# Letting a planned decoder kernel choose its engine for standardisation and for the addends of maxima

## The chip, the core and the metric

The kernel runs on one core of a Trainium2 chip. The metric is the device time of one execution in microseconds (us); lower is better. The core has five engines that run at the same time and meet through semaphores: TensorE (PE, with its weight loads PEld), VectorE (DVE), ScalarE (ACT), GpSimd (POOL) and SyncE (SP), whose queue issues this kernel's DMA transfers. Matrix products land in PSUM[...].

## The reference, cut to what matters

Two sequences of 512 tokens with 1024 features pass through three blocks, each with a layer normalisation ahead and a residual around it:

```python
x = x + attn(layernorm(x), ...)    # 32 heads over 8 kv heads; weights are signs times a scale; full softmax
x = x + xattn(layernorm(x), ...)   # see below
x = x + ffn(layernorm(x), ...)     # dense 1024x1024 plus low-rank products
```

```python
def rat_read(res, W, gamma, beta, num_outputs):
    x = res.reshape(b, l, H, C)                     # 256 x 4
    y = jnp.einsum('blhc,hoc->bloh', x, W)          # 3 or 2 outputs of 256
    mu = y.mean(-1, keepdims=True)
    var = y.var(-1, keepdims=True)
    yn = (y - mu) * jax.lax.rsqrt(var + EPS)        # standardisation
    return yn * gamma + beta
# xattn: rat_read (3) -> rotated causal attention, 16 heads -> rat_write (gated state update)
#        -> rat_read (2) -> silu(gate) * up -> rat_write
```

Softmax needs the maximum of each row of scores. Both attentions of each sequence are therefore made in two passes: one that finds the maxima, one that makes exponentials of the shifted scores.

## The kernel before

The work is cut into jobs, each a Python generator. A job yields `(engine, time, ready)` ahead of a group of instructions, and the planner `run` picks the job whose step can start soonest, with a `lag` added to each job's time. That fixes one order of instructions per engine, written out before anything runs: a late operand holds up what stands behind it on the same engine. The lags of jobs are in the list in `build`, those of their spawned parts in `LAGS`. `self.free[engine]` is the planned time at which an engine comes free, and some steps look at it to choose between two engines, as `emptied` does. `take` and `give` hand out rooms of a fixed number of buffers: two single PSUM banks, three PSUM pairs, four `probs`, eight pages, eleven rows, twelve slabs.

The stages, named as the tiles are (A and B, and C and D, are the two sequences):

- `in`, `k`, `v`, `q`, `wo`, `proj`: the input tiles are standardised and split into three bf16 parts, the weights turned to signs, and q, k and v projected.
- `maxA`, `maxB`: the first attention's maxima, 8 groups of 4 heads. `peaks` makes the scores of 128 queries in two PSUM pairs, and `reduced` takes the maxima of each pair on VectorE (two reductions per step).
- `turned`, once per group, splits the maxima `mx` into three bf16 addends in `parts`. TensorE transposes `parts`, and ScalarE copies them out as `shift`. In `attend`, a matmul with a constant row of ones (`ones16`) adds the shift into the scores ahead of the exponential. So the maxima can be subtracted by TensorE.
- `attA`, `attB` (`attend_1`), `outA`, `outB`: exponentials on ScalarE, products with v, sums of exponentials. For the sums, VectorE adds the four tiles of exponentials of a group into `held`, and four matmuls with `ones` sum over keys. Where VectorE is planned to be more than `SPARE` us late at the end of a group, the last tile is not added but gets its own four matmuls (`direct`).
- `factor`: low-rank products for the last block, kept in DRAM.
- `stateA`, `stateB` (`state_inputs`): each tile of 128 tokens is read back, measured (`measured`: statistics on VectorE, the inverse deviation by a logarithm and an exponential on ScalarE), standardised over 1024 features and passed to `read`, which transposes, multiplies, and standardises three times over 256. The mean and deviation are kept in `norm` for the tails.
- `maxC`, `maxD`, `attC`, `attD`: the causal attention in the same two passes, 4 groups each.
- `tailA`, `tailB` (`tails`): the state update, a second `read` with two outputs, the gated product, a second update, per tile of 128 tokens, at most three tiles at a time. `tailW` loads their weights.
- `weights`, `factorsB`, `denseA`, `denseB`: the last block.

Standardisation before, in `state_inputs` and in `read`:

```python
t = yield "DVE", 1.3, t
nc.vector.tensor_scalar(x, x, mv[:, 0, 0:1], r, ALU.subtract, ALU.mult)
...
t = yield "DVE", 0.42 * nout, t
for o in range(nout):
    nc.vector.tensor_scalar(rows[o], rows[o], mv[:, o, 0:1], rstd[:, o : o + 1], ALU.subtract, ALU.mult)
```

Nearly all instructions of VectorE, ScalarE and GpSimd carry line 51 in the profile (the helper that records them), and most matmuls line 130, so groups are told apart by their tiles.

Of the kernel before, what the change touches and what calls it, by code (L numbers as in the profile page):

```python
# [22 lines left out]
D = 1024  # L23
# [46 lines left out]
class Kernel:  # L70
# [79 lines left out]
    def constants(self):  # L150
        nc = self.nc
        self.ident = self.const([P, P], "ident")
        make_identity(nc, self.ident)
        self.ident16 = self.const([P, P], "ident16", BF16)
        nc.vector.tensor_copy(self.ident16, self.ident)
        self.ones = self.const([P, P], "ones")
        nc.gpsimd.memset(self.ones, 1.0)
        self.ones16 = self.const([P, P], "ones16", BF16)
        nc.gpsimd.memset(self.ones16, 1.0)

        self.late = []
        for i, sign in enumerate((1, -1)):
            m = self.const([P, P], f"late{i}", BF16)
            nc.gpsimd.memset(m, 0.0)
            nc.gpsimd.affine_select(
                out=m, in_=m, compare_op=ALU.is_ge, fill=-1e30,
                base=0, pattern=[[-sign, P]], channel_multiplier=sign,
            )
            self.late.append(m)
        self.parts = [self.const([P, NT, 4, 32], f"parts{i}", BF16) for i in range(2)]  # L170
        for t in self.parts:
            nc.gpsimd.memset(t, 0.0)
        self.flip = 0
# [248 lines left out]
    def output_weights(self):  # L422
# [7 lines left out]
        "added": 0.0, "ahead": 0.0, "attA.ahead": -0.1, "attA.exponentials": -0.1, "attA.finished": 0.3,  # L430
        "attB.added": 0.0, "attB.ahead": -0.3, "co.emptied": -0.1, "cv.emptied": -0.1, "denseA.summed": -0.6,
        "denseB.emptied": 0.3, "denseB.summed": -2.0, "emptied": -0.6, "exponentials": 0.3,
        "factor.put": -1.0, "finished": 0.0, "gained": -1.0, "gated": -1.0, "joined": -0.6, "k.scale_of": 0.0,
        "maxA.reduced": 0.0, "maxA.turned": -0.1, "maxB.reduced": 0.3, "maxB.turned": -0.3,
        "maxD.turned": -0.3, "outA.clean": 1.0, "outA.stored": 2.0, "outB.stored": -1.0,
        "proj0.featured": -1.0, "proj0.valued": -0.6, "proj1.featured": -1.0, "proj1.valued": -0.6,
        "q.scale_of": 0.0, "residual": 1.0, "rotated": 0.0, "stateA.emptied": -0.3, "stateA.rotated": -0.1,
        "stateB.gained": 0.0, "stateB.rotated": 0.0, "stored": 0.6, "summed": -0.6, "tableB.emptied": -2.0,
        "tailA.gained": -1.0, "tailA.residual": -2.0, "tailB.gated": -0.3, "tailB.residual": 0.0,
        "v.scale_of": 0.0, "wo.scale_of": 0.0,  # L440
    }
    SPARE = 3

# [144 lines left out]
    def turned(self, name, b, g, mx, reduced, earlier):  # L588
        nc = self.io
        yield from self.join(*earlier)  # L590
        t = yield from self.join(*reduced)
        t = yield "DVE", 1.2, t
        parts = self.parts[self.flip]
        self.flip = 1 - self.flip
        rest = self.small([P, NT, 4], "rest")
        nc.vector.tensor_scalar(parts[:, :, :, 0], mx, -1.0, None, ALU.mult)
        nc.vector.scalar_tensor_tensor(rest, mx, -1.0, parts[:, :, :, 0], ALU.mult, ALU.subtract)
        nc.vector.tensor_copy(parts[:, :, :, 1], rest)
        nc.vector.tensor_tensor(parts[:, :, :, 2], rest, parts[:, :, :, 1], ALU.subtract)
        room = yield from self.take("bank")  # L600
        t = yield "PE", 0.35, max(t, room)
        turns = self.bank([P, NT, P], BF16)
        for qt in range(NT):
            self.turn_block(turns[:, qt, :], parts[:, qt].rearrange("p j i -> p (j i)"), self.ident16)
        room = yield from self.take("shift")
        t = yield "ACT", 0.59, max(t, room)
        shift = self.sb.tile([P, S], BF16, tag="shift", name=self._name("shift"), bufs=8)
        nc.scalar.copy(shift, turns.rearrange("p a b -> p (a b)"))
        self.give("bank", t)
        self.shifts[b][g] = shift  # L610
        self.when[f"{name}.{g}"] = t
        return t

    def attend(self, groups, operands, scale, causal):
# [4 lines left out]
        nc = self.io  # L619
# [19 lines left out]
        def probabilities(g, kt):  # L639
            if kt == 0:  # L640
                ops[g] = yield from operands(g)
            q, k, _, shift, ready, release, _ = ops[g]
            q0 = kt * P if causal else 0
            room = yield from self.take("pair", 2)
            rp = yield from self.take("probs")
            t = yield "PE", 1.46 * width[kt] + (0.1 if causal else 0.0), max(ready, room)
            s = self.scores(
                lambda j: k(j, kt * P, (kt + 1) * P), lambda j: q(j, q0, S), slice(q0, S), False
            )
            for j in range(4):  # L650
                r = slice(32 * j, 32 * j + 3)
                self.mm(
                    s[j // 2][:, j % 2, q0:], lhsT=self.ones16[r, :], rhs=shift[r, q0:], start=False, stop=True
                )
            if kt == NT - 1:
                release(t)
                self.give("shift", t)
            p = self.probs([P, 4, S])
            return p, self.spawn(exponentials(p, s, q0, max(t, rp)))
# [44 lines left out]
        for n, (g, kt) in enumerate(steps):  # L704
# [273 lines left out]
    def measured(self, parts, t):  # L978
# [13 lines left out]
        nc.scalar.activation(r, r, AF.Exp, scale=-0.5)  # L992
        return mv, r, t

    def read(self, x, t, w, gb, nout, dst, wide):


        nc = self.io
        n = nout * 32
        kind = "row" if nout == 2 else "page"  # L1000
        if wide:
# [13 lines left out]
            t = max(t, first)  # L1015
# [36 lines left out]
            self.give("page", done)  # L1052
        rows = [yn[:, o].rearrange("p a c h -> p (a c h)") for o in range(nout)]
        mv, rstd, t = yield from self.measured([[r] for r in rows], t)
        t = yield "DVE", 0.42 * nout, t
        for o in range(nout):
            nc.vector.tensor_scalar(
                rows[o], rows[o], mv[:, o, 0:1], rstd[:, o : o + 1], ALU.subtract, ALU.mult
            )
        yn = yn.rearrange("p o a c h -> p (o a c h)")  # L1060
        per = 8 if wide else 4
        ends = []
# [42 lines left out]
    def state_inputs(self, b, wide):  # L1105
# [10 lines left out]
        def tile_of(q):  # L1116
# [2 lines left out]
            x = self.page([P, D])  # L1119
            t = yield from self.fetch(x, self.kept[b][q][:, :], 512, max(ready, room))  # L1120
            mv, r, t = yield from self.measured([[x[:, :512], x[:, 512:]]], t)
            t = yield "DVE", 1.3, t
            nc.vector.tensor_scalar(x, x, mv[:, 0, 0:1], r, ALU.subtract, ALU.mult)
            keep = self.small([P, 2], "norm", bufs=8)
            nc.vector.tensor_copy(keep[:, 1:2], r)
            nc.vector.tensor_scalar(keep[:, 0:1], mv[:, 0, 0:1], r, -1.0, ALU.mult, ALU.mult)
            self.norm[b][q] = keep
            t = yield from self.read(
                x, max(t, weights), self.wr1, self.gb1, 3, lambda c: ys[c // 2][:, c % 2, q * P : (q + 1) * P], wide
# [526 lines left out]
    def build(self):  # L1656
# [31 lines left out]
                ("attA", self.attend_1(0, "maxA"), 0.0, "maxA.0"),  # L1688
                ("maxB", self.peaks_1(1), 0.0, "attA.scores"),
                ("outA", self.output_1(0), 0.0, "attA", "wo", "co"),  # L1690
                ("attB", self.attend_1(1, "maxB"), -1.0, "maxB"),
                ("tableA", self.rotation_table(0), 0.5, "attB.1"),
                ("tableB", self.rotation_table(1), 0.0, "attB.3"),
                ("stateW", self.state_weights(), 3.0, "attB.5"),
                ("outB", self.output_1(1), 0.5, "attB"),
                ("stateA", self.state_inputs(0, True), 0.2, "attB.scores"),
                ("maxC", self.peaks_2(0, "stateA"), 0.5, "stateA"),
                ("stateB", self.state_inputs(1, False), 0.5, "outB"),
                ("factor", self.factors(), -0.5, "maxB.3"),
                ("attC", self.attend_2(0, "maxC"), 0.2, "maxC.0"),  # L1700
                ("factorsB", self.factors_back(), 0.2, "attD"),
                ("maxD", self.peaks_2(1, "stateB"), 0.5, "stateB", "attC.scores"),
                ("tailW", self.tail_weights(), -0.5, "attC", "stateB"),
                ("tailA", self.tails(0), 0.5, "attC", "tailW"),
                ("attD", self.attend_2(1, "maxD"), 0.2, "maxD.1"),
                ("weights", self.dense_weights(), 0.2, "attD", "attC"),
                ("tailB", self.tails(1), 0.0, "attD", "tailW"),
                ("denseA", self.dense_all(0, "tailA"), 0.5, "tailA.0"),
                ("denseB", self.dense_all(1, "tailB"), 0.2, "tailB.0"),
            ]  # L1710
# [105 lines left out]
```

## Time and profile before

| | |
|---|---|
| median of 3 runs | 1136.23 us (1135.48 to 1136.71) |
| the profiled execution | 1135.51 us, of which the span from first to last instruction is 1133.8 us |
| mean granted TensorE clock | 0.965 |
| PE, PEld busy | 1063.1 us (94%), 521.5 us (46%) |
| DVE, ACT, POOL busy | 841.2 us (74%), 442.8 us (39%), 239.2 us (21%) |
| DMA | 70.51 MB, mean 62 GB/s |
| stages (from the trace) | maxA to 215, attA to 300, maxB with outA and factor to 430, attB to 535, stateA and outB to about 610, maxC and stateB to 662, attC and stateB to 725, maxD to 785, tails and dense to 1134 |

A time is compared with the profiled execution's own 1135.51 us. Busy shares are averages over stages with different limits: a stage's own windows say which engine fills it. "Idle before, and what ended it" names the operation that came last before an engine could go on. The granted clock is a share of full TensorE speed: where it is 0.9, a matmul takes longer than elsewhere.

### The profile page before, as it was taken

The numbers are of one execution on the slowest core, as the hardware profiler recorded it, in microseconds if no ns is written. First come the engines' busy times: TensorE is split into PE (matmuls) and PEld (weight loads), VectorE is DVE, ScalarE is ACT, GpSimd is POOL, SyncE is SP. The second block draws the span as 40 slices with busy tenths as digits, with TensorE's granted clock in tenths as the row PEclk, the third lists the DMA queues.
The fourth block names the chain that finished last, engine by engine and source line by source line (L and its number), as shares of the span: only waits on it lengthen the run. The fifth ranks groups of instructions, "written<-read, shape, count | busy, mean of one in ns | idle before, by whom it ended". The sixth has DMA issues, their size and how long they took to land.

```text
span 1133.8 us, 16121 instructions
## 1 busy us (share of the span) xinstructions
PE 1063.1 (94%) x6364; PEld 521.5 (46%) x6364; DVE 841.2 (74%) x1390; ACT 442.8 (39%) x711; POOL 239.2 (21%) x249
## 2 busy tenths in 40 slices
PE   4889999999999998999999899989988899999998
PEld 3554353333233632332555543545465465665643
DVE  7978888578878865887777961599668677788572
ACT  6762101388500215786221255224743232332310
POOL 3442333322222303454451012001200000000000
PEclk9999999999998997999999889979998999999999
DMA  6621000101214221240113000410151001011110
GB/s 256 203 82 28 20 10 20 29 20 29 61 33 177 95 64 39 61 168 1 38 56 116 8 11 16 172 38 1 57 197 68 33 20 55 11 48 38 38 37 38
DMA packets 24784, 70.51 MB, mean 62 GB/s; under 512 B 5234, under 2 KB 5252, under 8 KB 23684
## 3 DMA queue, kind: packets, MB, share of 16 engines
q1 hardware_dynamic: 24708, 69.48, 17.9%
q8 instruction: 50, 0.82, 0.3%
q14 instruction: 26, 0.21, 0.1%
HBM read 50.59 MB, written 10.49 MB: 54 GB/s over the span
## 4 chain that ended last, share of the span: by engine, by line
PE 79%; DVE 11%; ACT 5%; issue 2%; DMA 1%; POOL 1%; SPq 0%; ACTq 0%; DVEq 0%; POOLq 0%
PE proj_bank L130 8%; PE denseA_pair L130 6%; PE denseB_pair L130 6%; PE attA_pair L130 4%; PE outA_bank L130 4%; PE attB_pair L130 4%; PE tailB_bank L130 3%; PE attB_bank L130 3%; PE attA_bank L130 3%; PE maxB_pair L130 3%; PE maxA_pair L130 3%; PE tailA_bank L130 3%; PE outB_bank L130 3%; PE stateB_bank L130 3%; PE tailB_pair L130 3%; PE tailA_pair L130 3%
## 5 line engine op out<-in xcount | busy, mean ns | idle before, releaser
L51 DVE TENSOR_REDUCE maxB_mx<-maxB_pair 128x2 f32<-128x1024 f32 x64 | 75.3, 1217 | 21.7 <-PE maxB_pair L130 21.3
L51 DVE TENSOR_REDUCE maxA_mx<-maxA_pair 128x2 f32<-128x1024 f32 x64 | 75.5, 1216 | 14.0 <-PE maxA_pair L130 14.0
L130 PEld LDWEIGHTS <-start_slab 128*128 128x128 bf16 x480 | 44.7, 98 | 68.8 <-issue 21.1
L51 DVE TENSOR_TENSOR attB_probs<-attB_probs,attB_probs 128x1024 f32<-128x1024 f32 x46 | 62.6, 1401 | 13.8 <-PE attB_bank L130 13.5
L51 ACT ACTIVATE attB_probs<-attB_pair 128x1024 f32<-128x1024 f32 x64 | 62.6, 1023 | 20.9 <-PE attB_pair L130 10.8
L51 DVE TENSOR_TENSOR attA_probs<-attA_probs,attA_probs 128x1024 f32<-128x1024 f32 x46 | 56.6, 1282 | 16.9 <-PE attA_bank L130 8.5
L51 ACT ACTIVATE attA_probs<-attA_pair 128x1024 f32<-128x1024 f32 x64 | 62.1, 1021 | 9.7 <-PE attA_pair L130 9.4
L130 PE MATMUL proj_bank<-in_slab,start_slab 128*128 128x512 bf16 x240 | 55.5, 379 | 1.7 <-ACT in_slab L51 1.7
L130 PE MATMUL proj_bank<-in_probs,start_slab 128*128 128x512 bf16 x240 | 54.7, 380 | 0.0
L130 PE MATMUL maxB_pair<-maxB_row,proj_slab 32*128 32x512 f32 x256 | 47.4, 687 | 3.1 <-DVE maxB_mx L51 3.1
L51 POOL TENSOR_SCALAR proj_row<-proj_row 128x512 f32<-128x512 f32 x24 | 47.7, 1987 | 1.9
L130 PE MATMUL outA_bank<-wo_slab,attA_slab 128*128 128x512 bf16 x192 | 46.7, 392 | 0.7 <-ACT maxB_shift L51 0.7
L130 PE MATMUL attB_pair<-proj_slab,attB_row 32*128 32x512 f32 x256 | 46.7, 685 | 0.0
L51 ACT ACTIVATE proj_row<-proj_bank,cs 128x512 f32<-128x512 f32 x20 | 13.7, 686 | 80.8 <-PE proj_bank L130 60.2
L130 PE MATMUL outB_bank<-wo_slab,attB_slab 128*128 128x512 bf16 x192 | 43.3, 379 | 0.3 <-POOL attB_slab L51 0.3
L130 PE MATMUL attA_pair<-proj_slab,attA_row 32*128 32x512 f32 x256 | 41.6, 639 | 0.3 <-ACT attA_probs L51 0.3
L51 POOL MEMSET tailB_row<- 9x128 f32 x8 | 1.6, 195 | 186.4 <-PE tailB_bank L133 70.7
L130 PE MATMUL attB_bank<-attB_probs,proj_slab 128*32 128x512 f32 x256 | 38.4, 633 | 1.1 <-DVE tableA_slab L51 0.7
L51 ACT COPY maxB_shift<-maxB_bank 128x512 bf16<-128x512 bf16 x8 | 4.7, 586 | 84.7 <-PE maxB_bank L133 84.7
L51 POOL TENSOR_SCALAR proj_slab<-proj_row 128x512 f32<-128x512 f32 x24 | 14.9, 621 | 106.6 <-ACT proj_row L51 89.0
L130 PE MATMUL maxA_pair<-maxA_row,proj_slab 32*128 32x512 f32 x256 | 36.8, 640 | 0.0
L51 POOL TENSOR_SCALAR_AFFINE_SELECT attD_probs<-attD_probs 128x512 f32<-128x512 f32 x16 | 12.1, 754 | 113.8 <-ACT attD_probs L51 104.3
(410 smaller groups left out, 2321.8 us busy)
## 6 DMA issues: line engine op xcount, KB each, us to landing
in_page<-in_x_dram SPq DMA_DIRECT2D x8, 512.0 KB, 4.1
q_page<-in_q_weight_dram SPq DMA_DIRECT2D x8, 512.0 KB, 5.3
wo_page<-in_o_weight_dram SPq DMA_DIRECT2D x8, 512.0 KB, 3.4
tailW_slab<-in_write_dram SPq DMA_DIRECT2D x3, 752.0 KB, 7.1
maxA_row<-proj_slab SPq DMA_DIRECT2D x32, 64.0 KB, 2.0
attA_row<-proj_slab SPq DMA_DIRECT2D x32, 64.0 KB, 2.0
maxB_row<-proj_slab SPq DMA_DIRECT2D x32, 64.0 KB, 2.0
outA_page<-in_x_dram SPq DMA_DIRECT2D x4, 512.0 KB, 3.7
```

The source lines that it names most:

```text
L51: return self.kernel.pin(getattr(self.engine, name)(*args, **kw))
L130: self.pin(self.nc.tensor.matmul(*args, **kw))
```

## The change

Five things are changed at once:

1. `standard`, a new step, standardises on VectorE if the plan has it free no later than 0.5 us after ScalarE or the data, and else on ScalarE, after GpSimd has made the product -mean times inverse deviation (`off`). `state_inputs` and `read` use it; the inputs' `split_tile` and `dense` do not.
2. The two small operations that keep `norm` go from VectorE to GpSimd.
3. `turned` runs on VectorE or GpSimd, whichever the plan would finish sooner. The addends are no longer negated; the constant rows hold -1 instead of 1 (`minus16`).
4. `SPARE` goes from 3 to 1.
5. Several lags, and the events after which jobs may start, are new.

```diff
-        self.ones16 = self.const([P, P], "ones16", BF16)
-        nc.gpsimd.memset(self.ones16, 1.0)
+        self.minus16 = self.const([P, P], "minus16", BF16)
+        nc.gpsimd.memset(self.minus16, -1.0)
...
-        "factor.put": -1.0, ... "stateA.emptied": -0.3, "stateA.rotated": -0.1,
-        ... "tailB.residual": 0.0,
+        "factor.put": -2.0, ... "stateA.emptied": -0.3, "stateA.gained": -0.6,
+        ... "tailA.emptied": -1.0, ... "tailB.residual": -2.0,
     }
-    SPARE = 3
+    SPARE = 1
...
-        t = yield "DVE", 1.2, t
+        by, cost = min(("DVE", 0.9), ("POOL", 1.2), key=lambda e: self.free[e[0]] + e[1])
+        t = yield by, cost, t
+        e = nc.vector if by == "DVE" else nc.gpsimd
...
-        nc.vector.tensor_scalar(parts[:, :, :, 0], mx, -1.0, None, ALU.mult)
-        nc.vector.scalar_tensor_tensor(rest, mx, -1.0, parts[:, :, :, 0], ALU.mult, ALU.subtract)
-        nc.vector.tensor_copy(parts[:, :, :, 1], rest)
-        nc.vector.tensor_tensor(parts[:, :, :, 2], rest, parts[:, :, :, 1], ALU.subtract)
+        e.tensor_copy(parts[:, :, :, 0], mx)
+        e.tensor_tensor(rest, mx, parts[:, :, :, 0], ALU.subtract)
+        e.tensor_copy(parts[:, :, :, 1], rest)
+        e.tensor_tensor(parts[:, :, :, 2], rest, parts[:, :, :, 1], ALU.subtract)
...
+    def standard(self, parts, n, t):
+        nc = self.io
+        if self.free["DVE"] <= max(self.free["ACT"], t) + 0.5:
+            t = yield "DVE", (0.15 + n / 1500) * len(parts), t
+            for x, mean, r in parts:
+                nc.vector.tensor_scalar(x, x, mean, r, ALU.subtract, ALU.mult)
+        else:
+            t = yield "POOL", 0.2 * len(parts), t
+            off = self.small([P, 3], "off")
+            for i, (x, mean, r) in enumerate(parts):
+                nc.gpsimd.tensor_scalar(off[:, i : i + 1], mean, r, -1.0, ALU.mult, ALU.mult)
+            t = yield "ACT", (0.2 + n / 1310) * len(parts), t
+            for i, (x, mean, r) in enumerate(parts):
+                nc.scalar.activation(x, x, AF.Identity, scale=r, bias=off[:, i : i + 1])
+        return t
...
-            t = yield "DVE", 1.3, t
-            nc.vector.tensor_scalar(x, x, mv[:, 0, 0:1], r, ALU.subtract, ALU.mult)
             keep = self.small([P, 2], "norm", bufs=8)
-            nc.vector.tensor_copy(keep[:, 1:2], r)
-            nc.vector.tensor_scalar(keep[:, 0:1], mv[:, 0, 0:1], r, -1.0, ALU.mult, ALU.mult)
+            yield "POOL", 0.4, t
+            nc.gpsimd.tensor_copy(keep[:, 1:2], r)
+            nc.gpsimd.tensor_scalar(keep[:, 0:1], mv[:, 0, 0:1], r, -1.0, ALU.mult, ALU.mult)
+            t = yield from self.standard([(x, mv[:, 0, 0:1], r)], D, t)
...
-                ("attB", self.attend_1(1, "maxB"), -1.0, "maxB"),
-                ("tableA", self.rotation_table(0), 0.5, "attB.1"),
+                ("attB", self.attend_1(1, "maxB"), 0.5, "maxB.3"),
+                ("tableA", self.rotation_table(0), 1.0, "attB.1"),
...
-                ("stateW", self.state_weights(), 3.0, "attB.5"),
-                ("outB", self.output_1(1), 0.5, "attB"),
-                ("stateA", self.state_inputs(0, True), 0.2, "attB.scores"),
+                ("stateW", self.state_weights(), 0.0, "attB.3"),
+                ("outB", self.output_1(1), 0.0, "attB"),
+                ("stateA", self.state_inputs(0, True), 0.2, "attB.7"),
...
-                ("attC", self.attend_2(0, "maxC"), 0.2, "maxC.0"),
-                ("factorsB", self.factors_back(), 0.2, "attD"),
+                ("attC", self.attend_2(0, "maxC"), 0.0, "maxC.0"),
+                ("factorsB", self.factors_back(), 0.2, "attD", "attC"),
...
-                ("tailW", self.tail_weights(), -0.5, "attC", "stateB"),
+                ("tailW", self.tail_weights(), 8.0, "attC", "stateB"),
...
-                ("attD", self.attend_2(1, "maxD"), 0.2, "maxD.1"),
-                ("weights", self.dense_weights(), 0.2, "attD", "attC"),
-                ("tailB", self.tails(1), 0.0, "attD", "tailW"),
+                ("attD", self.attend_2(1, "maxD"), 0.2, "maxD", "attC"),
+                ("weights", self.dense_weights(), -0.5, "attD", "attC"),
+                ("tailB", self.tails(1), 0.0, "attD", "tailW", "tailA.0"),
```

`attB.3`, `attB.7` and the like are set when that group's first product with v is planned, `attB.scores` when the last scores are, and `maxB.3` when the shift of the fourth group is ready.

More of the change, by code (lines that the diff above doesn't have):

```diff
@@ L432 @@
         "denseB.emptied": 0.3, "denseB.summed": -2.0, "emptied": -0.6, "exponentials": 0.3,
-        "factor.put": -1.0, "finished": 0.0, "gained": -1.0, "gated": -1.0, "joined": -0.6, "k.scale_of": 0.0,
+        "factor.put": -2.0, "finished": 0.0, "gained": -1.0, "gated": -1.0, "joined": -0.6, "k.scale_of": 0.0,
         "maxA.reduced": 0.0, "maxA.turned": -0.1, "maxB.reduced": 0.3, "maxB.turned": -0.3,
@@ L436 @@
         "proj0.featured": -1.0, "proj0.valued": -0.6, "proj1.featured": -1.0, "proj1.valued": -0.6,
[L437 to L440, printed above, removed]
+        "q.scale_of": 0.0, "residual": 1.0, "rotated": 0.0, "stateA.emptied": -0.3, "stateA.gained": -0.6,
+        "stateA.rotated": -0.1, "stateB.gained": 0.0, "stateB.rotated": 0.0, "stored": 0.6, "summed": -0.6,
+        "tableB.emptied": -2.0, "tailA.emptied": -1.0, "tailA.gained": -1.0, "tailA.residual": -2.0,
+        "tailB.gated": -0.3, "tailB.residual": -2.0, "v.scale_of": 0.0, "wo.scale_of": 0.0,
     }
-    SPARE = 3
+    SPARE = 1
     def run(self, jobs):
@@ L652, in probabilities @@
                 self.mm(
-                    s[j // 2][:, j % 2, q0:], lhsT=self.ones16[r, :], rhs=shift[r, q0:], start=False, stop=True
+                    s[j // 2][:, j % 2, q0:], lhsT=self.minus16[r, :], rhs=shift[r, q0:], start=False, stop=True
                 )
@@ L1054, in read @@
         mv, rstd, t = yield from self.measured([[r] for r in rows], t)
[L1055 to L1059, printed above, removed]
+        t = yield from self.standard([(rows[o], mv[:, o, 0:1], rstd[:, o : o + 1]) for o in range(nout)], 256, t)
         yn = yn.rearrange("p o a c h -> p (o a c h)")
```

## The prediction

> **What bounds the kernel now.** The page's first and second parts come first: which engine is busy, and where it is not.
>
> ```profile
> PE 1063.1 (94%) x6364; PEld 521.5 (46%) x6364; DVE 841.2 (74%) x1390; ACT 442.8 (39%) x711; POOL 239.2 (21%) x249
> PEclk9999999999998997999999889979998999999999
> PE 79%; DVE 11%; ACT 5%; issue 2%; DMA 1%; POOL 1%; SPq 0%; ACTq 0%; DVEq 0%; POOLq 0%
> ```
>
> TensorE bounds as a whole. What can be won is its idle time and the time at a lower granted clock. The chain confirms it: VectorE holds 11% of it, so it ends some waits. Next come the windows by stage (start:end, length, then busy us of PE, PEld, DVE, ACT, POOL, then the clock):
>
> ```profile
> 215.00:300.00 85.00, 84.73 (x704) 27.21 (x701) 64.91 (x61) 74.18 (x86) 19.10 (x21) 1.00 0.11 29
> 300.00:430.00 130.00, 123.11 (x584) 51.01 (x580) 104.92 (x152) 13.58 (x22) 30.45 (x33) 0.94 0.26 88
> 430.00:535.00 105.00, 102.87 (x748) 31.93 (x749) 77.39 (x69) 77.72 (x93) 47.58 (x49) 0.94 0.22 72
> 535.00:610.00 75.00, 72.29 (x348) 39.79 (x347) 58.56 (x122) 13.46 (x39) 35.67 (x28) 1.00 0.16 57
> 610.00:662.00 52.00, 47.23 (x342) 30.55 (x342) 46.03 (x103) 15.09 (x38) 0.00 (x0) 0.90 0.12 42
> 725.00:785.00 60.00, 53.09 (x358) 30.79 (x356) 52.54 (x108) 21.64 (x40) 1.57 (x2) 0.89 0.05 18
> 860.00:920.00 60.00, 52.43 (x221) 28.20 (x220) 46.39 (x94) 16.00 (x35) 0.39 (x2) 0.89 0.05 18
> ```
>
> A stage's pool, the most it can give back, is length minus PE busy, plus PE busy times (1 - clock). attA (215 to 300) has 0.3 us. maxB beside outA and the factors (300 to 430) has 6.9 + 7.4 = 14.3, attB (430 to 535) 2.1 + 6.2 = 8.3, stateA beside outB 2.7, maxC beside stateB (610 to 662) 4.8 + 4.7 = 9.5, maxD beside tailA (725 to 785) 6.9 + 5.8 = 12.7, and 860 to 920 has 7.6 + 5.8 = 13.4. In maxC and maxD, VectorE is about as busy as TensorE while ScalarE and GpSimd stand nearly idle: there taking work off VectorE can shorten the run. In attA it can't. The waits of TensorE name the same culprit:
>
> ```profile
> PE maxD_pair L130 <- DVE maxD_mx L51: 3.9, 5, 2.2
> PE maxB_bank L133 <- DVE parts L51: 3.4, 1, 3.4
> PE maxC_bank L133 <- DVE parts L51: 1.3, 1, 1.3
> ```
>
> **The change, part by part.**
>
> (a) *Addends of the maxima* (`turned`, 24 groups). VectorE runs four small operations, 0.20, 0.18, 0.20 and 0.23 us in the rows of `parts`, 0.81 us per group and 19 us in all. The new code keeps four, without negation (the constant rows of minus one absorb it, at the same matmul count), on VectorE or GpSimd. No row shows them on GpSimd. From below: the 128x1 memsets of `rot_page` took 99 ns, so 0.4 us per group. From above: the 128x128 copies:
>
> ```profile
> L51 POOL COPY tableA_row<-rotations x12: 291/298/301, 438.1 to 440.7; 128x128 f32<-128x128 f32 x12
> L51 POOL COPY tableB_row<-rotations x12: 292/1014/1289, 478.3 to 492.3; 128x128 f32<-128x128 f32 x12
> ```
>
> so 1.2 us undisturbed, and 4.1 at the median beside attB's additions. The Trainium skill (SBUF — State Buffer, Who interferes with whom) says that a VectorE instruction with two SBUF inputs and a reading GpSimd instruction shut each other out for a whole instruction, and that a reduction never does. The second row agrees with its first half. By the rule, groups that meet attB's additions cost 4.1 us of delay, the others about 1. Taken: 1.0 in maxC and maxD, 3 beside attB. On GpSimd they queue behind outA's cleaning (two operations, 1.34 us each in the mean); behind the transposition of `parts`, which waits for them in TensorE's fixed order, stand the next scores, and behind those the reductions. What covers the delay is that maxB leads attB by four groups and that the plan may place the transposition late; without that cover, 1 to 3 us of TensorE standing per group. Relief of VectorE: 3.2 us in maxC, 3.2 in maxD.
>
> (b) *Kept constants* (`norm`): 0.146 + 0.202 us leave VectorE per tile, 8 tiles, 2.8 us. They go to GpSimd, and only the tails read them, some 100 us later. Price 0 to 0.4 us on GpSimd, hidden.
>
> (c) *Standardisation.* 8 passes of 128x1024 in the state inputs, 24 of 128x256 behind their first read, 16 in the tails. VectorE's rows are 0.81 and 0.40 us; stateA's narrow ones mean 0.64, beside a GpSimd busy 35.67 of 75 us. On ScalarE the same shape stands in the trace: tailB_slab with scale and bias from `norm`, 1.237 us; for 128x256 it is at most the gain's 0.46 us for 128x128 plus the difference of copies, about 0.57 (copies: 0.59 us at 512, 0.37 at 256). The skill speaks against this: ScalarE: Activation LUTs, Rules for kernel authors, wants add and multiply on VectorE, not ScalarE. Rows and rule agree on the price: 0.43 us slower for the wide pass, and a GpSimd product (0.1 to 0.3 us) and two hand-overs of about 0.1 come first, so +0.8 us of latency. Behind the waiting pass in ScalarE's queue stand the emptyings of banks (`stateB_page`, 0.59 us), for which TensorE's next transposition waits. By the rule, with a handful (6) of these on the path, it costs 5 us and wins nothing. By the windows VectorE is full in 610 to 662 (46.03 of 52) while ScalarE has 15.09, so the pass waits longer for VectorE than it loses. I follow the windows, and take half as moved: in stateB half of 4 x 0.81 + 12 x 0.40 = 8 us, in stateA half of 10.9, in the tails half of 0.8 us per tile.
>
> (d) *SPARE 3 to 1.* Where VectorE is planned over 1 us late at a group's end, the last addition (two of 1.22 to 1.40 us) is replaced by four more matmuls with `ones`, 1.04 us of TensorE. In attA the last multiplication of a group ends about when VectorE ends the addition before (269.06 and about 269.1 us), so few groups should switch: one or two, all exposed, +1. In attB, sharing VectorE with maxB, about four; half hidden where VectorE bounds: +2.
>
> (e) *Order.* attB may start after `maxB.3` instead of all of maxB. Now TensorE stands 3.4 us at 426.9 for VectorE's last reductions and `parts`, and the slice 420 to 440 has a clock of 0.73 on 16.6 busy us: 4.5 us more. attB's scores can fill this: 7.9 us at most, I take 7. stateA starts at `attB.7`, stateW and outB sooner; their stage has a pool of 2.7, I take 1. attD waits for all maxima and for attC: before it began at 771.3, and the last `parts` are read at 777.6, so up to 6 us of filler is lost in maxD's stage; the tails cover most, +1. tailW's lag 8 moves its loads (eleven transfers: weights, du and bias of the first part, `read2`, `gain2`, `ctx` twice, two of weights, du and bias of the second) behind others on SP's queue. Before, ctx was issued at 705.9 and first read at 773.8: over 60 us of slack hide 8. Uncovered it is 8 us. The first part's weights were issued at 619.7 and first read at 724.8. Behind them on SP stand only `tailA_slab`'s rows (711.6), which can pass them now. The new lags of `factor.put`, `gained`, `emptied`, `residual` only reorder: 0, bounds -3 to +3.
>
> *Sum by stage.* maxB and attB: -7 + 2 = -5. stateA: -1. maxC and stateB: relief 3.2 + 4 + 0.7 (half the `norm` pairs of 1.4), 7.9 of VectorE's 46; TensorE's own full-clock need is 42.5 of 52, so the limit is 9.5, and about half arrives because the chain of one tile stays: -5. maxD and tailA: relief 3.2 + 0.8, of which three quarters: -3, +1 for attD: -2. attA +1. Tails and dense, pool of some 31 after 785, relief 8 x 0.4 = 3.2: -2. That is -14; a new order also makes waits that no row shows, for which I give 2 back: -12. The profiled execution took 1135.5 us (span 1133.8 and 1.7 around it): 1123.5, and 0.7 more for the median, 1136.2: **1124 us**. A measurement of this kernel can tell about 0.2% (2.3 us) from no change.
>
> **Rivals.**
>
> *Slower: the three PSUM pairs.* maxB and attB each take two of three at a time. The 16 last steps of maxB would run beside attB. One round holds pairs for 2.3 + 3.5 us (scores 1.06, reductions 1.22 each) and 2.9 + 3.9 (scores 1.9, exponentials 1.02 each): 12.6, by three 4.2 us, against 3.5 of TensorE work. So 0.7 us per round, 16 rounds: +11, and the 7 us of the join don't come: -12 + 7 + 11 = +6, 1142; at a whole reduction per round, 19 us, 1150. It decides from 0.3 us per round ((12 - 7)/16). For it: TensorE already waits for `maxD_mx`. Against: outA and the factors, in other banks, fill.
>
> *Hidden.* The relief falls where TensorE is full anyway and the join is only moved: -1, 1135. For it: attA, attB and stateA are at 96 to 100% of TensorE.
>
> *The switch hardly switches.* The plan finds VectorE free and all stays; only the order acts, -7 + 2 - 1 + 1 + 1 - 2 = -6, 1130. Against: in maxC it is the busiest.
>
> *More.* If half of the 31 us after 785 goes too, -28: 1108.
>
> **How the numbers follow.** Main 0.42 and the unswitched 0.12 are faster, as is More, 0.12: 0.66. Hidden 0.06: same. Pairs, or a like wait in the new order, 0.28: slower. The range 1104 to 1148 leaves out about 0.06 below and 0.12 above; the likeliest case alone spans 1112 to 1132.
>
> **What would show it.** Right: `parts` rows on POOL in maxB to maxD, ACT rows with `stateB_mv`'s `off` scalars; 610 to 662's work in under 48 us at a clock over 0.93; no 3 us wait for `parts` at maxB's end; a few more than 72 `ones` records per attention. Wrong: TensorE waits for `maxB_mx` or `attB_probs` above 10 us, a lower clock in attB, or late loads before the first tail.

## The result and the profile after

The changed kernel takes 1164.3 us in the median of its runs (1161.75 to 1165.86) against 1136.2: 2.5% slower, ratio 1.0251 with a 95% interval of 1.0228 to 1.0274. The forecast, 1124 (1104 to 1148), was on the wrong side. The profiled execution took 1161.75 us, of which the span is 1160.0.

First the same rows of the page: busy time, granted clock by slice.

```profile
PE 1065.7 (92%) x6364; PEld 522.7 (45%) x6364; DVE 818.6 (71%) x1280; ACT 454.6 (39%) x729; POOL 280.9 (24%) x362
PEclk9999999999998999999979899878999999999899
```

TensorE does the same work in nearly the same busy time (1063.1 before), so of the 26.2 us that the span grew all but 2.6 are idle time. VectorE gave 22.6 us away and TensorE still waits longer. The page's chain of waits covers only the last quarter of this span, so the next view is that of windows, cut at the stages of the new order (start:end, length, busy us of PE, PEld, DVE, ACT, POOL, then the clock, the DMA share and GB/s):

```profile
300.00:430.00 130.00, 122.75 (x600) 51.16 (x592) 98.65 (x125) 13.56 (x22) 36.91 (x56) 0.97 0.24 84
430.00:531.00 101.00, 96.74 (x732) 30.30 (x728) 76.91 (x68) 76.72 (x92) 54.03 (x54) 0.97 0.22 70
531.00:646.00 115.00, 99.13 (x469) 56.53 (x466) 72.29 (x150) 34.95 (x82) 46.02 (x56) 0.94 0.18 63
646.00:691.00 45.00, 43.75 (x281) 21.52 (x283) 36.67 (x61) 6.51 (x16) 3.25 (x13) 0.92 0.03 7
733.00:793.00 60.00, 45.87 (x282) 24.24 (x283) 43.14 (x83) 16.50 (x31) 4.78 (x20) 0.76 0.22 87
```

Two stages carry the loss. From outB to the end of stateA (531 to 646) TensorE has 16 idle us. Before, the same stretch was 26 us shorter, with 4 idle us:

```profile
533.00:622.00 89.00, 84.92 (x412) 47.93 (x408) 67.23 (x141) 18.26 (x50) 35.94 (x29) 1.00 0.17 59
```

So about 12 of the 26 us are idle time and 14 are busy time. Of the busy time, 9 us are matmuls of stateB that now fall into this stretch (13.1 busy us of `stateB_bank` instead of 4.1); the rest goes with the clock, 0.94 instead of 1.00. From 733 to 793 (maxD) TensorE is idle for 14 us, at a clock of 0.76. TensorE's waits and ScalarE's longest new one name the places (us in total, times, longest):

```profile
PE tailA_bank L133 <- ACT tailA_row L51: 11.1, 3, 7.6
PE stateB_bank L133 <- ACT stateB_page L51: 5.1, 1, 5.1
PE maxD_bank L133 <- POOL parts L51: 3.9, 1, 3.9
PE maxB_bank L133 <- POOL parts L51: 1.7, 1, 1.7
ACT stateA_page L51 <- POOL stateA_off L51: 28.6, 3, 14.2
```

The first of these was small before:

```profile
PE tailA_bank L133 <- ACT tailA_row L51: 1.7, 2, 1.4
```

The switch of engines did happen. The rows of `parts` on GpSimd (duration in ns, min/median/max), four operations per group:

```profile
L51 POOL CAST parts<-maxB_mx x7: 252/642/663, 326.4 to 430.1; 128x16 bf16<-128x16 f32 x7
L51 POOL CAST parts<-maxC_mx x4: 253/254/255, 657.5 to 690.8; 128x16 bf16<-128x16 f32 x4
L51 POOL TENSOR_TENSOR maxC_rest<-maxC_mx,parts x4: 227/228/232, 657.8 to 691.1; 128x16 f32<-128x16 f32 x4
L51 POOL CAST parts<-maxC_rest x4: 252/254/747, 658.1 to 691.4; 128x16 bf16<-128x16 f32 x4
L51 POOL TENSOR_TENSOR parts<-maxC_rest,parts x4: 267/267/268, 658.5 to 692.2; 128x16 bf16<-128x16 f32 x4
```

All groups of maxC and maxD, 7 of 8 in maxB and 4 of 8 in maxA went to GpSimd. Five of the eight wide standardisations, and 16 of the 40 narrow ones, went to ScalarE. `SPARE` switched nothing: the page still has 46 additions in attA and 46 in attB, as before.

What did change most is the order on TensorE. The timeline from attB's end (start us, busy us, group, and in brackets the idle time before it), before:

```profile
538.94 2.98 PE L130 MATMUL outB_bank<-wo_slab,attB_slab 128*128 128x512 bf16 x13 [0.34 <-POOL attB_slab L51]
541.76 1.04 PE L133 MATMUL stateA_pair<-ident,stateA_page 128*128 128x128 f32 x8
542.63 1.46 PE L130 MATMUL outB_bank<-wo_slab,attB_slab 128*128 128x512 bf16 x6
543.93 1.92 PE L130 MATMUL stateA_pair<-read,stateA_probs 128*128 128x96 f32 x16
545.69 1.04 PE L133 MATMUL stateA_pair<-ident,stateA_page 128*128 128x128 f32 x8
```

and after:

```profile
531.66 5.14 PE L130 MATMUL outB_bank<-wo_slab,attB_slab 128*128 128x512 bf16 x23
537.19 36.65 PE L130 MATMUL outB_bank<-wo_slab,attB_slab 128*128 128x512 bf16 x169 [0.39 <-POOL attB_slab L51]
573.68 1.91 PE L133 MATMUL stateA_pair<-ident,stateA_page 128*128 128x128 f32 x16
...
583.28 1.67 PE L133 MATMUL stateA_pair<-ident,stateA_probs 128*128 128x128 f32 x6 [2.00 <-ACT stateA_probs L51]
585.23 1.51 PE L133 MATMUL stateA_pair<-ident,stateA_probs 128*128 128x128 f32 x6 [0.28 <-DVE stateA_probs L51]
591.86 1.97 PE L133 MATMUL stateB_bank<-ident,stateB_page 128*128 128x128 f32 x8 [5.12 <-ACT stateB_page L51]
```

All 192 products of outB run as one block. Before, stateA's first transposition stood after 36 of them, at 541.8, and its steps alternated with the rest; now it stands at 573.7, and the chain transpose, read, measure, standardise, transpose has nothing beside it until stateB's first transposition at 591.9.

Milestones, as the first or last start of an instruction that writes or reads the tile in each trace (us):

| | before | after |
|---|---|---|
| attB's last use of its exponentials | 532.9 | 531.1 |
| stateA's last use of its banks | 621.8 | 646.2 |
| stateB's | 724.3 | 712.9 |
| attC's last `probs` | 708.7 | 733.2 |
| maxD's last maxima | 774.0 | 786.0 |
| attD's first and last `probs` | 773.4, 836.3 | 792.9, 857.8 |
| span | 1133.8 | 1160.0 |

Read downwards: 24 us are lost by stateA's end. Some of stateB's work had already been done in that stretch (91 matmuls of `stateB_bank` instead of 30), so both sequences are through (stateB and attC) only 9 us late. From there to maxD's end 3 more go, to attD's end 9.5 more, and 4.7 behind it.

### The profile page after: what moved, and what is told of

Same layout as the page of the kernel before. It is cut to its first block, busy times and chain, and to the rows that moved or that the text cites. A ratio compares the mean times of both kernels' runs of the same rounds, so it can differ in the third digit from the quotient of the medians.

```text
span 1160.0 us, 16120 instructions
## 1 busy us (share of the span) xinstructions
PE 1065.7 (92%) x6364; PEld 522.7 (45%) x6364; DVE 818.6 (71%) x1280; ACT 454.6 (39%) x729; POOL 280.9 (24%) x362
## 5 line engine op out<-in xcount | busy, mean ns | idle before, releaser
L51 DVE TENSOR_TENSOR attA_probs<-attA_probs,attA_probs 128x1024 f32<-128x1024 f32 x46 | 56.7, 1282 | 16.9 <-PE attA_bank L130 10.6
L130 PE MATMUL maxB_pair<-maxB_row,proj_slab 32*128 32x512 f32 x256 | 43.5, 651 | 1.6 <-DVE maxB_mx L51 1.6
L130 PE MATMUL attB_pair<-proj_slab,attB_row 32*128 32x512 f32 x256 | 44.2, 652 | 0.2 <-DVE maxB_mx L51 0.2
L130 PEld LDWEIGHTS tailA_pair<-tailA_row,tailW_probs 128*128 128x128 f32 x256 | 32.1, 207 | 5.8 <-issue 3.1
L130 PE MATMUL attA_bank<-attA_probs,proj_slab 128*32 128x512 f32 x256 | 34.1, 605 | 0.0
L130 PE MATMUL tailA_pair<-tailA_row,tailW_probs 128*128 128x128 f32 x256 | 33.5, 294 | 0.6 <-DVE tailA_row L51 0.5
```

The source lines that it names most:

```text
L51: return self.kernel.pin(getattr(self.engine, name)(*args, **kw))
L130: self.pin(self.nc.tensor.matmul(*args, **kw))
```

## The experiments

All ratios are to the kernel before, run on the same chip, with 95% intervals. "New engines" are GpSimd's addends and kept constants and ScalarE's standardisations. An order means what the planner writes for TensorE and SP's queue.

### First four: one part of the change at a time, planned anew

In the first (e1), the changed kernel gets back all the lags, `SPARE` and the job list of before; in the second (e2), the kernel before gets those of the change. Each edit lets the planner draw its order again.

```diff
-    SPARE = 1
+    SPARE = 3
...
-                ("outB", self.output_1(1), 0.0, "attB"),
+                ("outB", self.output_1(1), 0.5, "attB"),
...
```

> The changed kernel with the lags, SPARE and job list of before: only the free choice of engines, the kept constants on GpSimd and the unnegated addends remain. Theory (a lag of 0.0 puts outB ahead of stateA, so all 192 matmuls of outB run as one block and nothing is left to cover stateA's chains): about 1130, between 1122 and 1138, since outB and stateA alternate again and VectorE is relieved. Rival (the constants and products of stateA queue on GpSimd behind outB's cleaning): 1150 to 1165, because that queue is the same.

Measured: 1162.0 us, 1.0229 (1.0209 to 1.0249). To 725 us it is level with before (stateB's end 725.6); the whole loss comes behind it.

> The kernel of before, with nothing but the new lags, SPARE and job list; all standardisation, constants and addends stay on VectorE. Theory (order): 1160 to 1172, stateA ends some 20 us later than before although GpSimd has nothing of it. Rival (GpSimd's queue): 1130 to 1145.

Measured: 1204.1 us, 1.0603 (1.0580 to 1.0626).

The third (e3) is the changed kernel with one lag of before:

```diff
-                ("outB", self.output_1(1), 0.0, "attB"),
+                ("outB", self.output_1(1), 0.5, "attB"),
```

> The changed kernel with one number put back: the lag of outB is 0.5 again instead of 0.0. Theory (order): most of the loss goes, 1130 to 1145; stateA's last matmul near 622 to 628 us instead of 646. Rival (GpSimd's queue): 1155 to 1164, the waits of ScalarE for stateA_off stay above 10 us.

Measured: 1197.5 us, 1.0552 (1.0534 to 1.0570).

The fourth (e4) is the changed kernel with the wide pass and the kept constants of the state inputs on VectorE again:

```diff
-            yield "POOL", 0.4, t
-            nc.gpsimd.tensor_copy(keep[:, 1:2], r)
...
+            t = yield "DVE", 1.3, t
+            nc.vector.tensor_scalar(x, x, mv[:, 0, 0:1], r, ALU.subtract, ALU.mult)
```

> The changed kernel with the 1024-wide standardisation and the kept constants of the state stage back on VectorE; the order's numbers stay. Theory (order): 1158 to 1168, outB still one block. Rival (GpSimd's queue): 1135 to 1148.

Measured: 1206.5 us, 1.0623 (1.0607 to 1.0639).

Each theory missed by over 20 us the runs that should have brought its gain back: e1 and e3 for outB's lag, e4 and e2 for GpSimd's queue. (In e1 the rival's range of 1150 to 1165 was met, but not in the stage that it spoke of.) The stage itself is clear. From outB's first product to stateA's last, the traces have 88.3 us before, 89.8 in e1 and 91.4 in e3, where outB and stateA alternate; and 114.5 after, 114.0 in e2 and 119.4 in e4, where outB is one block. So outB's lag of 0.0, which puts all its products ahead of stateA's, costs 25 us in that stage, with new or old engines there; a single lag (e3) takes 23 of them back. ScalarE's wait for GpSimd, 28.6 us in the changed kernel, is not what makes the stage long: in e2 GpSimd has no part of the standardisation, and the stage is as long. The totals could not show it, since each edit redrew the tails as well, and worse. The next runs therefore hold the order.

### The order held: what the new engines cost

In e6 and e7 only the engine that is written changes; the planner still reckons with the old ones, so TensorE and SP's queue keep the order of before. e6 moves the addends and the kept constants, e7 also the eight wide passes.

```diff
         t = yield "DVE", 1.2, t
...
-        nc.vector.tensor_scalar(parts[:, :, :, 0], mx, -1.0, None, ALU.mult)
+        e = nc.vector if name == "maxA" else nc.gpsimd
+        e.tensor_copy(parts[:, :, :, 0], mx)
...
```

and in e7, in `state_inputs`:

```diff
-            nc.vector.tensor_scalar(x, x, mv[:, 0, 0:1], r, ALU.subtract, ALU.mult)
+            nc.scalar.activation(x, x, AF.Identity, scale=r, bias=keep[:, 0:1])
```

> The kernel before with its plan, lags and order untouched, but the addends of maxB, maxC and maxD and the kept constants are written to GpSimd at the same places (minus16 as in the change; the planned engines and costs are not changed, so TensorE's order is that of before). Theory 'order': the engines of these small operations are worth little either way; the 28 us come from the new order. Expects 1128 to 1139, TensorE's waits for parts each under 4 us and their sum within 5 us of before's. Rival 'engines': the addends on GpSimd, 1.0 to 1.4 us per group behind cleaning, hold up the transpositions of parts and all scores behind them. Expects 1142 to 1165, with a group of waits for POOL parts of 10 us or more.

Measured: 1137.4 us, 1.0027 (1.0012 to 1.0042). VectorE is busy 12.5 us less (828.7), and no stage is shorter: maxC's maxima run from 622.6 to 663.6 (622.9 to 663.8 before), maxD's from 724.3 to 773.5 (724.9 to 774.0). TensorE's waits for the addends in e6, which were 3.4 and 1.3 us on VectorE:

```profile
PE maxB_bank L133 <- POOL parts L51: 4.4, 1, 4.4
PE maxC_bank L133 <- POOL parts L51: 2.1, 1, 2.1
```

Each is 0.8 to 1.0 us longer. That is the length of the addends' own chain: from the first start to the last end, the four operations of a group take 0.92 us on VectorE before, and 1.23 to 1.92 us on GpSimd in e6.

> As the run before, and also all eight wide standardisations of stateA and stateB go to ScalarE behind a GpSimd product (the kept constant serves as the bias), again with the plan and the order of before. Theory 'order': +0.8 us of latency per tile beside outB's products and stateB's chain, at most 6 of 8 exposed: within -3 to +6 us of the run with the addends alone, 1128 to 1144. Rival 'engines': ScalarE's queue, with the emptyings of banks behind the waiting pass, is what the changed kernel lost in stateA: +10 to +25 us over the addends alone.

Measured: 1140.3 us, 1.0054 (1.0029 to 1.0079), 0.3% or 3 us beyond e6; the two intervals overlap, so this difference is barely clear of the noise. In the trace it lies in stateA, which ends at 626.9 instead of 621.5 in e6 (1.7 of these 5.4 us are there before outB starts); the wide pass takes 1.24 us on ScalarE.

e13 moves in addition the narrow passes of stateA and both tails, in `read`:

```diff
...
+                nc.gpsimd.tensor_scalar(off[:, o : o + 1], mv[:, o, 0:1], rstd[:, o : o + 1], -1.0, ALU.mult, ALU.mult)
...
+                nc.scalar.activation(rows[o], rows[o], AF.Identity, scale=rstd[:, o : o + 1], bias=off[:, o : o + 1])
```

> The order of before on TensorE and SP's queue, with all the changed kernel's kinds of engine change at once and more of each: addends of maxB to maxD and kept constants on GpSimd, the eight wide standardisations and the narrow ones of stateA and of both tails (28 of 40) on ScalarE behind GpSimd's product. Theory 'order': the wide ones cost 0.3% beyond the addends; 20 narrow steps at 0.8 us of latency, of which TensorE's neighbours cover two thirds, add 2 to 7 us: 1141 to 1149. Rival 'engines': the tails' chains of one tile are on the path, so 16 steps of 0.8 us or more arrive in full: 1153 to 1170.

Measured: 1142.2 us, 1.0068 (1.0045 to 1.0090). The narrow passes add no more than the measurement can tell. With more work moved than the change moves in standardisation (only maxA's addends stay on VectorE), all new engines together cost 8 us at the order of before.

### The order alone

e15 is the changed kernel, planned alike to the last step, with every instruction of the changed parts written to VectorE:

```diff
-        e = nc.vector if by == "DVE" else nc.gpsimd
+        e = nc.vector
...
-                nc.scalar.activation(x, x, AF.Identity, scale=r, bias=off[:, i : i + 1])
+                nc.vector.tensor_scalar(x, x, mean, r, ALU.subtract, ALU.mult)
```

> The changed kernel's order on TensorE and on SP's queue to the last instruction, with every addend, kept constant and standardisation written to VectorE at the place that the plan gave it elsewhere. Theory 'order': the 28 us stand in the order alone, and the engines are worth 0.3 to 0.6% as at the fixed order of before: 1155 to 1172. Rival 'engines in this order': the new engines' latency in the uncovered stages makes most of the loss, and taking it away brings 1140 to 1152.

Measured: 1176.2 us, 1.0364 (1.0334 to 1.0393). Both expectations were wrong here: each had the new engines cost time in this order. The run completes a table of four, as ratios to before:

| | old engines | new engines |
|---|---|---|
| order of before | 1 | 1.0068 (e13) |
| order of the change | 1.0364 (e15) | 1.0251 (the change) |

The order costs 3.6% with the old engines. In it, the new engines win back 1.1%, some 13 us, and that is where the prediction's relief of VectorE is found. In e15 stateA ends at 651.5 instead of 646.2, and maxD's maxima at 797.1 instead of 786.0. In stages that the new order had left uncovered, work taken off VectorE shortens the run; in the order of before the same moves won nothing (e6, e7, e13).

### Is it this order, or any other?

e8 is the kernel before with one planned cost changed and no instruction:

```diff
-        t = yield "DVE", 1.2, t
+        t = yield "DVE", 0.9, t
```

> The kernel before with one number of the plan changed: the planned cost of the addends of the maxima on VectorE, 1.2 to 0.9. No instruction is added, removed or moved to another engine, but the planner draws another order. Theory 'order': the lags of before fit one drawing of the plan, and another drawing with the same lags loses tens of us in the tails: 1145 to 1210, with the loss behind 725 us. Rival 'engines': a redrawn order is about as good, 1130 to 1142, and only the new engines' latency costs.

Measured: 1154.2 us, 1.0170 (1.0146 to 1.0194). A number that only the planner reads moves the time by 19 us. The place was not as expected: 8 us are gone at attB's start (441.5 instead of 433.4), where outA's last products now wait for VectorE behind maxB:

```profile
PE outA_bank L130 <- DVE outA_row L51: 8.9, 3, 4.6
```

and most of the rest is lost between maxD and the first dense products.

e9 and e10 are the kernel before, with all its lags, plus one planned choice of engine: `standard` and the kept constants in e9, `turned` in e10 (the diff's lines, unchanged).

> The kernel before with its lags, SPARE, list of jobs and its addends on VectorE, plus only the part on standardisation and kept constants as the change has it (chosen by the plan). Theory 'order': the plan is redrawn from stateA on, so it loses like the run with all new engines in the old lags (1162): 1145 to 1200, in stages that have no standardisation on ScalarE on TensorE's waits. Rival 'engines': the loss is where ScalarE standardises, in stateA and stateB (535 to 725): these stages are over 8 us longer than before, the tails not.

Measured: 1176.3 us, 1.0365 (1.0335 to 1.0396). tailA's last products come by 981 instead of 1092 us, and denseB starts at 1045.5 instead of 985.0: the last sequence runs its tails alone. In e9, 985 to 1045:

```profile
985.00:1045.00 60.00, 47.13 (x194) 27.73 (x192) 48.39 (x96) 17.28 (x34) 0.19 (x1) 0.81 0.03 9
```

Before, TensorE was busy for 59.05 of these 60 us, at full clock. e14 keeps that order and writes the standardisation and the kept constants to VectorE:

```diff
-                nc.scalar.activation(x, x, AF.Identity, scale=r, bias=off[:, i : i + 1])
+                nc.vector.tensor_scalar(x, x, mean, r, ALU.subtract, ALU.mult)
```

> The order of the run that changed only the standardisation's plan (1176), with its standardisations and kept constants written to VectorE at the same places. Theory 'order': the tails finish tailA by 981 us and then run tailB alone, which leaves TensorE idle from 985 to 1045 whatever engine standardises: 1166 to 1182. Rival 'engines': ScalarE's pass in tailB's chain is what TensorE waits for there: 1140 to 1158.

Measured: 1181.9 us, 1.0411 (1.0381 to 1.0442), and 45.26 busy us in the same window: so the order, not ScalarE, leaves TensorE idle there.

> The kernel before with its lags, SPARE, list of jobs, standardisation and kept constants, plus only the planned choice of VectorE or GpSimd for the addends of the maxima. The instructions themselves cost 0.3% at a fixed order. Theory 'every redrawn order loses with lags of another plan': 1145 to 1180, as the other redrawn orders did (1154 to 1206), with the loss behind 725 us. Rival 'the standardisation's and the new lags' orders are the bad ones; a redrawn order may fall either way': 1122 to 1140, stateA between outB's products as before, tails from maxD's start to the end within 409 +- 8 us.

Measured: 1134.3 us, 0.9987 (0.9976 to 0.9998). The theory that every redrawn order loses was wrong, and the rival right: here the redrawn order is about as good as the old one. Its 1.5 us are the only gain among all versions, and hardly more than the noise. maxB's last maxima come 3.7 us sooner (425.8) and attD ends 9 us sooner (827.1 instead of 836.3); the stages behind attD give most of it back. So a redrawn order isn't bad as such; it is a draw.

### Two prices measured by themselves

e11 does the addends of maxC and maxD twice, in `turned`, at the order of before:

```diff
+        if name in ("maxC", "maxD"):
+            nc.vector.tensor_scalar(parts[:, :, :, 0], mx, -1.0, None, ALU.mult)
...
```

> The kernel before, order untouched, with the four addend operations of each of the eight groups of maxC and maxD done twice on VectorE (0.8 us more per group, 3.2 us per stage). The prediction's step 'VectorE bounds maxC and maxD, so half to three quarters of its relief arrive' makes this 1139 to 1143, with maxC's stage (622.9 to 663.8 before) and maxD's (724.9 to 774.0) 2 to 3 us longer each. Rival 'VectorE is busy there but not what TensorE waits for': within 1.5 us of before, both stages within 1 us.

Measured: 1143.6 us, 1.0079 (1.0061 to 1.0098): 9 us for 6.5 us of added work. maxC's last maxima come 3.5 us later than before; maxD's stage, 54.2 us, is 5.1 longer:

```profile
725.00:785.00 60.00, 54.60 (x313) 30.59 (x312) 48.51 (x113) 16.40 (x31) 1.21 (x2) 0.74 0.05 20
```

Its clock is 0.74, where it was 0.89. Work added to the chain of reductions, addends, transposition costs more than its length here. Taken off VectorE (e6) it returns nothing: the addends are still in that chain, and longer in it.

e12 goes for the changed kernel's wait of 7.6 us at 740. ScalarE's timeline there, after:

```profile
736.05 0.63 ACT L51 ACTIVATE attC_row<-attC_row 128x512 f32<-128x512 f32 x1
744.12 3.71 ACT L51 ACTIVATE tailA_slab<-tailA_slab,stateA_norm 128x1024 f32<-128x1024 f32 x3 [7.44 <-DMA tailA_slab<-kept]
747.74 0.35 ACT L51 COPY tailA_row<-tailA_bank 128x256 f32<-128x256 f32 x1
```

and SP's queue:

```profile
728.54 2.90 SPq L142 DMA_DIRECT2D tailW_probs<-in_ctx_dram  x2
731.55 0.84 SPq L142 DMA_DIRECT2D tailW_slab<-in_write_dram  x2
...
733.35 1.96 SPq L142 DMA_DIRECT2D tailA_slab<-kept  x3
```

The loads of `ctx` wait for attC to free `probs`, and the tiles' rows stand behind them and land at 744. e12 takes their buffers and issues three of them first, in `tail_weights`; `tails` and `tail` then leave these steps out:

```diff
+        yield from self.take("slab", 2)
+        self.x[0] = [self.slab([P, 2, D]) for _ in range(2)]
+        for q in range(3):
+            self.load(self.tokens(0, q), self.kept[0][q][:, :])
         yield from self.take("probs", 2)
         self.ctx = [self.probs([P, 2, D]) for _ in range(2)]
```

> The changed kernel with one thing moved: the loads of the first three tiles of tailA_slab are issued ahead of the two of ctx on SP's queue, which wait for attC's last reads of probs. The order on the four computing engines stays. Theory 'late rows': TensorE's wait of 11.1 us for tailA_row around 740 goes, and the run is 5 to 10 us faster, 1154 to 1159. Rival 'nothing to fill': what TensorE waits for there is also ctx and the second part's weights themselves, or the chain of the tails' first tile; the wait moves to the next step and the run stays within 2 us of 1164.

Measured: 1152.7 us, 1.0158 (1.0143 to 1.0173), 0.9% or 10.6 us less than the changed kernel. The 7.6 us wait is gone, and the same 60 us now hold

```profile
733.00:793.00 60.00, 52.48 (x376) 30.85 (x371) 51.30 (x94) 22.46 (x41) 6.17 (x22) 0.89 0.18 69
```

with the clock back from 0.76 to 0.89. attD ends at 848.3 instead of 857.8, so the late rows make most of what the changed kernel loses between the end of stateB and attC and the end of attD. outB's block has no such run: none takes it back while the rest of the order is held, so its 9 us of the total are read from the milestones.

## Why the prediction was wrong, point by point

**The failed step is (e), the order.** The prediction took each stage's pool as what a new order could give back, and never priced what an order can take: the work that stood beside a chain. "stateA starts at attB.7, stateW and outB sooner; their stage has a pool of 2.7, I take 1" was entered as a gain. It measured +26 us from outB's start to stateA's end; the next stretch, to the end of stateB and attC, is 15 us shorter, since part of stateB was done by then. The small pool should have been the warning: TensorE was 96% busy there because outB's products covered stateA's chain, and the diff put outB's lag at 0.0.

**"tailA_slab's rows (711.6), which can pass them now"** had the queue the wrong way round. tailA's job starts only when tailW's is through, so its rows always stand behind ctx. The lag of 8 itself does nothing: with -0.5 the planner writes the same program. What made them late was the cover again: before, stateB's projections and rotations ran to 724.3, 16 us past attC; after, stateB was through 20 us before attC. Price 10.6 us (e12), where the text had 0, or 8 uncovered. The prediction did name late loads before the first tail as a sign that it was wrong.

**"only reorder: 0, bounds -3 to +3"** was the wrong size of bound for any change of order. No run takes these lags alone, but redrawn orders with the old lags gave -1.5 (e10), +19 (e8) and +42 us (e9).

**(a) and (c), the relief of VectorE,** did not arrive at the order of before (e6 +3 us), where half to three quarters of it had been taken. The step that failed is the reading of a window: VectorE busy for 46 of 52 us was taken as the bound, though the addends only change engine within one chain. What they cost there stands in no line of the sum, which has the relief alone. (a) names 1.0 us for a group on GpSimd in maxC and maxD; the trace has 1.23 to 1.81 from first start to last end (e6), against 0.92 on VectorE. The 3 us beside attB were not put to the test: the changed kernel's last group in maxB ends at 432.0, and attB's additions begin at 438.8. In the uncovered order the relief is real, 13 us (e15 against the change): right mechanism, on a path that the forecast didn't see.

**The rule against ScalarE** (the Trainium skill, ScalarE: Activation LUTs, Rules for kernel authors, as quoted in the forecast) fits the order of before: the eight wide passes cost some 3 us (e7 less e6), where the rule's working had 5 and the windows a gain. In the order of the change the balance is on the other side, since VectorE is what the chain waits for.

**(d)** was +3 and is 0; nothing switched (46 additions in each attention, before and after). **attB from maxB.3** was -7 and is -1.8 at attB's end: the wait for the last addends shrank from 3.4 us to 1.7 and 1.0, but the other idle time of that stretch stayed. **(b)** was hidden, as said, within e6's total.

Of the rivals, the slower one had the right side and the wrong mechanism: TensorE waits no longer for pairs than before. "Or a like wait in the new order" was put in as a word, without a place or a price, and that was the case. What stays open is how the last 5 us, behind attD, divide; and e8's loss behind maxD was not followed to its waits.

## What to carry to other kernels

Where instructions are laid out by a plan, a change of engine is also a change of order, and here the order was worth five times the engine (3.6% against 0.7%). First move the instruction with the order held, then hold the order and move it back, and only then look at the sum. A stage in which TensorE is nearly full may be full because a neighbour covers its chains; before pricing a lag by the idle time that it may win, ask what would stand beside each chain if the neighbour ran first. Loads that wait for a buffer set the time of everything behind them on their queue, so put the short ones that are needed first ahead of them.

## What the runs showed of the hardware

GpSimd's operations on 128x16 took 0.23 to 0.27 us in the changed kernel when VectorE was idle or in a reduction from PSUM. Those that started beside a running VectorE operation with two inputs in SBUF grew to as much as 0.77 us and ended about 0.1 us after it, as here in maxB:

```profile
326.25 0.72 DVE L51 COPY_PREDICATED outA_row<-outA_row,outA_row 128x512 f32<-128x512 int32 x1
326.40 0.65 POOL L51 CAST parts<-maxB_mx 128x16 bf16<-128x16 f32 x1 [3.81 <-DVE maxB_mx L51]
```

The median of 642 ns in maxB's first row above comes from this; (a) had read the same from the copies of `tableB_row` beside attB's additions.

The granted clock can fall behind gaps of quite different length. In the changed kernel it was 0.50 from 745 to 750, behind the wait of 7.6 us; in e12, without that wait, 1.00. In e11 the 3.4 us before 745 held no gap of TensorE above 0.6 us, with TensorE busy for 2.19 us of them, and the clock was 0.50 from 745 to 760. The idle time of e11's 60 us was not longer than before, 5.4 us against 6.9, so its mean clock of 0.74 can't be read from the length of the gaps alone; what decides it stays open.
